# Decoder layer, 16 batches on one core: from batch 4 on, x is transposed by VectorE in 32x32 blocks and put together by way of DRAM

## The chip, the core and the metric

The kernel runs on one core of a Trainium2 chip. A core has five engines with an instruction queue each: TensorE (PE, matrix products; its weight loads are listed apart as PEld), VectorE (DVE), ScalarE (ACT), GpSimd (POOL) and SyncE (SP, which here only starts transfers). Sixteen DMA engines move data between DRAM and the on-chip memory SBUF. Matrix products end in PSUM, which has eight banks of 512 fp32 columns in this kernel's use. The metric is the time on the device in microseconds (us), the median of several runs.

## The reference, cut to what matters

x has shape (16, 512, 256), everything is fp32. Each batch goes through linear attention, cross attention to 64 context rows with softmax, and a routed expert layer, each with a residual and a layer norm. What the change touches is the first of these:

```python
q  = x + x @ Wq + bq
ks = x + x @ Wk[k] + bk[k]            # k = 0, 1
vs = x + x @ Wv[k] + bv[k]
state = prod_k (ks[k].T @ vs[k])      # per head, 16 heads of 16 channels
out = layernorm(q @ state) @ Wo + bo
x   = layernorm(x + out)
```

The expert layer keeps, for each of 8 experts, the first 1024 tokens of non-zero routing weight. With weights that are all positive these are batches 0 and 1, whose expert work is laid in the main part of the kernel. The last loop of the kernel takes up further batches if a count made on the chip asks for it.

## The kernel before, in words

A batch of x has 512 tokens and 256 channels. It is used in three forms.

- `gx` (`load_gram_x`, L293): tokens on partitions, four tiles of 128 tokens, with a column of ones set by POOL (L296). `gram` (L550) takes x.T x from it (L555, L560), which is a sum over tokens. The two gram blocks go to SBUF by `evac` (L182), which takes ACT (L186) and DVE (L188) in turn, and one block is transposed by TensorE (L573). Two buffers of `gx` exist; `gram` of batch b starts the load of batch b + 2.
- `xt` (`load_x`, L609): tokens on partitions again, one buffer, loaded at the start of `self_attention` (L614), used as the residual.
- `xT`: channels on partitions, 512 tokens in the free dimension, one buffer, which `zT` of the same batch shares. It is the weight operand of z = x m (L687), where m is Wq times the state of this batch.

`xT` is made from `xt` by `transposed` (L227): for each of two halves of the channels, four 128x128 TensorE transposes into one PSUM bank (L233), then one copy of 128x512 to SBUF. So a batch has eight transposes and two copies, one on ACT and one on DVE. The same helper makes `x1T` for the cross attention, and the transposed heads for the experts.

The order of all work is written out ahead by a planner. Generators stand for streams: grams, context, self attention, cross attention, routing, experts. A stream gives up its turn by `yield`; by `yield WAIT` it asks not to be called before the model's time at which what it has issued is done. `weave` (L1010) always calls the ready stream whose planned time is earliest. A stream's planned time moves with the TensorE time that it has spent, by the class `Model` (L28), which keeps a clock for each engine. One step of 78 us is planned for each batch (L1071, L1084); the gram of a batch is planned 3.8 steps ahead of its self attention (L1056 and L1071). Experts fill what is left (L1117). The resulting order is fixed for TensorE, VectorE, ScalarE and GpSimd by `in_order` (L1029). Each engine therefore runs its own list in order and waits by semaphores; SP likewise starts transfers in the order in which they are written.

All transfers of the kernel before are started by SP. Among those beside the change: the eight value blocks `vo` of a batch, 32 transfers in all (L781), of which the last two blocks are asked for while the product with the probabilities (`ps_x`, L834) runs; the loads of `gx` (L299) and `xt` (L611); the value store (L497).

`w_all` holds the routing weights of all batches; `ranks` writes a masked copy into `w_sel` (L910), which only the last loop reads.

Of the kernel before, what the change touches and what calls it, by code (L numbers as in the profile page):

```python
# [9 lines left out]
FP = mybir.dt.float32  # L10
# [17 lines left out]
class Model:  # L28
# [37 lines left out]
    def run(self):  # L66
# [4 lines left out]
        for ins in traced[self.seen:]:  # L71
# [4 lines left out]
            for made, used, l in ((1, 0, names[0]), (1, 1, names[1])):  # L76
                for n in l:
                    if kind == "InstDMACopy" and self.made.get(n, (0, 0))[1] == "SP":
                        continue
                    for known, book in ((made, self.made), (used, self.used)):  # L80
                        if known and n in book:
                            t, by = book[n]
                            at = max(at, t + (self.WIDE.get(by, 0.0) if by != engine else 0.0))
            if kind == "InstDMACopy":
                size = 4 * min(a.size() for l in aps for a in l)
                start = max(at, self.dma if now < 40 else 0.0)
                self.dma = start + size / 220e3
                done = self.dma + 2.0
            elif names[1]:
                start = max(at, self.free.get(engine, 0.0))  # L90
                done = self.free[engine] = start + self.duration(ins, kind, engine)
                if engine == "PE":
                    self.took += done - start
                else:
                    end = max(end, done + 0.15)
            else:
                continue
            for n in names[0] + names[1]:
                self.used[n] = max(self.used.get(n, (0.0, None)), (done, engine), key=lambda p: p[0])
            for n in names[1]:  # L100
                self.made[n] = (done, engine)
        self.seen, self.end = len(traced), end
# [14 lines left out]
def decoder_layer(  # L117
# [41 lines left out]
    HEAD_B = CAP // S  # L159
    GB = 2  # L160
    QB = 4
    CX = C + E
# [55 lines left out]
    NTT = B * NT  # L218
    w_sel = const.tile([P, NTT, E], FP, tag="w_sel", name="w_sel")
    n_i = const.tile([P, 1], I32, tag="n_i", name="n_i")  # L220
# [6 lines left out]
    def transposed(dst, src, view=lambda t: t, ones=False):  # L227


        for cc in range(NC):  # L230
# [3 lines left out]
            v = view(dst[:, cc, :])  # L234
            ps = ps if len(v.shape) == 2 else ps.rearrange("p (q t i) -> p q t i", q=NT, t=NT)
            if ones and cc == NC - 1:
                nc.vector.tensor_scalar(v, ps, not_last, ident[:, P - 1:P], ALU.mult, ALU.add)
            elif ones:
                nc.scalar.copy(v, ps)
            else:  # L240
                evac(v, ps)

    def moments(NT=NT):
# [28 lines left out]
    with ExitStack() as att:  # L272
# [19 lines left out]

        def load_gram_x(b, eng=nc.sync, pieces=1):  # L293

            t = gp.tile([P, NT, C + 1], FP, tag="gx", name="gx")
            nc.gpsimd.memset(t[:, :, C:], 1.0)  # L296
            n_ = NT // pieces
            for i in range(pieces):
                eng.dma_start(  # L299
                    out=t[:, i * n_:(i + 1) * n_, :C],  # L300
                    in_=x[b, i * n_ * P:(i + 1) * n_ * P, :].rearrange("(t p) c -> p t c", p=P),
                )
            return t

        gram_x = {0: load_gram_x(0, pieces=NT)}


# [142 lines left out]
        def context_keys():  # L450
# [27 lines left out]

            last = small.tile([P, NP], FP, tag="last", name="last")
            nc.vector.tensor_copy(last, xwq[:, :, C - 1])  # L480
# [69 lines left out]
        def gram(b, u4):  # L550
# [8 lines left out]
            for t in range(NT):  # L559
                nc.tensor.matmul(  # L560
                    ps[:, C + 1:C + P + 2], gx[:, t, P:C], gx[:, t, P:], start=(t == 0), stop=(t == NT - 1)
                )
            if b + 2 < B:
                gram_x[b + 2] = load_gram_x(b + 2)
            g = gp.tile([P, 4, P], FP, tag="g", name="g", bufs=5)
# [8 lines left out]
            evac(g[:, 3, :], ps[:, :P])  # L574
            grams[b] = g
            yield WAIT

# [28 lines left out]

        grams, sums = {}, {}

# [5 lines left out]
        def self_attention(b, done):  # L614
# [3 lines left out]
            sk = wk1.tile([P, K, NC, P], FP, tag="sk", name="sk")  # L618
            xT = wk1.tile([P, NC, S], FP, tag="xT", name="xT")
            gks = []  # L620

# [40 lines left out]
            nc.vector.scalar_tensor_tensor(state, state, STATE_SCALE, headmask, ALU.mult, ALU.mult)  # L662
            yield from until(lambda: made(xt))
            transposed(xT, xt)
            yield WAIT

# [13 lines left out]
            nc.scalar.copy(bq_state[:, :C], ps[:, :C])  # L680
            yield WAIT
            z = wk1.tile([P, NT, CX], FP, tag="z", name="z")
            mm = moments()
            for t in range(NT):
                ps = bank("ps_o")
                for cc in range(NC):
                    nc.tensor.matmul(  # L687
                        ps[:, :CX], xT[:, cc, t * P:(t + 1) * P], m[:, cc, :], start=(cc == 0), stop=(cc == NC - 1)
                    )
# [185 lines left out]
        def ranks():  # L875
# [33 lines left out]
            nc.vector.tensor_add(rank, rank, start)  # L909
            nc.vector.scalar_tensor_tensor(w_sel, rank, float(CAP), w_all, ALU.is_lt, ALU.mult)  # L910
            NB = B - HEAD_B
            least = small.tile([P, NB], FP, tag="least", name="least")
            nc.vector.tensor_reduce(
# [155 lines left out]
        def all_self_attention():  # L1069
            for b in range(B):  # L1070
                self_st.plan(SETUP + (b - 1) * STEP, STEP, 16.5)  # L1071
                yield from until(lambda: b in grams and sums[b // QB][1] and "rb" in cs and made(grams[b], sums[b // QB][1][0]))
                yield from self_attention(b, done)
# [86 lines left out]
    with tc.For_i(0, n, 1) as i:  # L1160
        acc = fw.tile([P, NT, C], FP, tag="acc", name="acc")
        nc.sync.dma_start(out=acc, in_=x2_rest[ds(i * S, S), :].rearrange("(t p) c -> p t c", p=P))
        wb = fw.tile([P, NT, E], FP, tag="wb", name="wb")
        nc.vector.tensor_copy(wb, w_sel[:, ds(i * NT + HEAD_B * NT, NT), :])
        aT = fw.tile([P, NC, S], FP, tag="aT", name="aT")
# [46 lines left out]
```

## Time and profile before

| | |
|---|---|
| median of 3 runs | 1387.47 us (1385.21 to 1389.51) |
| the profiled execution's own time | 1389.4 us |
| its span, first to last instruction | 1387.6 us |
| mean TensorE clock granted | 0.994 of full |
| ACT share of the span | 29% |
| DMA engines, mean busy share, all queues | about 41% |
| moved by DMA | 153.57 MB |

The profile shows one execution. An engine's busy time is the union of its instructions' durations. Consecutive matrix products overlap, so the duration of one is longer than the distance from its start to that of the next; that distance is read from the timeline. The chain of work that ended last is followed backward from the end: at each step to what released the instruction, or to its predecessor on the same engine.

### The profile page before, as it was taken

The numbers are of one execution on the slowest core, as the hardware profiler recorded it, in microseconds if no ns is written. First come the engines' busy times: TensorE is split into PE (matmuls) and PEld (weight loads), VectorE is DVE, ScalarE is ACT, GpSimd is POOL, SyncE is SP. The second block draws the span as 40 slices with busy tenths as digits, with TensorE's granted clock in tenths as the row PEclk, the third lists the DMA queues.
The fourth block names the chain that finished last, engine by engine and source line by source line (L and its number), as shares of the span: only waits on it lengthen the run. The fifth ranks groups of instructions, "written<-read, shape, count | busy, mean of one in ns | idle before, by whom it ended". The sixth has DMA issues, their size and how long they took to land.

```text
span 1387.6 us, 24209 instructions
## 1 busy us (share of the span) xinstructions
PE 1365.9 (98%) x9630; PEld 1077.9 (78%) x9630; DVE 850.7 (61%) x1957; ACT 402.2 (29%) x912; POOL 203.7 (15%) x140
## 2 busy tenths in 40 slices
PE   8999999999999999999999999999999999999997
PEld 5766576877878787878878787878888787878686
DVE  2445848466584848475584848475665939484744
ACT  1134224132232314142233323142323323232322
POOL 0001112112020111112020112112020202111200
PEclk9999999999999999999999999999999999999999
DMA  8657775511515153522606053513334061505211
GB/s 260 203 136 191 189 195 163 142 32 42 145 53 150 46 142 106 127 77 52 181 24 164 31 142 106 126 62 77 110 95 123 16 187 46 147 26 126 91 56 40
DMA packets 98372, 153.57 MB, mean 111 GB/s; under 512 B 15560, under 2 KB 70096, under 8 KB 98256
## 3 DMA queue, kind: packets, MB, share of 16 engines
q1 hardware_dynamic: 98256, 151.98, 40.1%
q8 instruction: 78, 1.28, 0.4%
q14 instruction: 38, 0.31, 0.1%
HBM read 114.71 MB, written 37.22 MB: 109 GB/s over the span
## 4 chain that ended last, share of the span: by engine, by line
PE 89%; DVE 5%; DMA 2%; SPq 1%; ACT 1%; issue 1%; ACTq 0%; DVEq 0%
PE ps_x L834 16%; PE ps_sim L814 15%; PE ps_e L963 15%; PE ps_h L946 15%; PE ps_gk L629 4%; PE ps_p L711 4%; PE ps_o L687 3%; PE ps_kv L437 3%; PE ps_t L233 2%; PE ps_kq L751 2%; PE ps_vo L492 2%; PE ps_s L641 2%; PE ps_g L555 2%; PE ps_zt L700 1%; PE ps_m L670 1%; PE ps_g L560 1%
## 5 line engine op out<-in xcount | busy, mean ns | idle before, releaser
L946 PE MATMUL ps_h<-head_T,wi 128*128 128x256 f32 x1024 | 239.1, 379 | 0.0
L834 PE MATMUL ps_x<-vo,pT 32*128 32x264 f32 x4096 | 234.9, 384 | 3.9 <-DVE pT L804 3.7
L814 PE MATMUL ps_sim<-kq,x1T 128*128 128x512 f32 x512 | 235.0, 593 | 0.0
L834 PEld LDWEIGHTS ps_x<-vo,pT 32*128 32x128 f32 x4096 | 211.5, 186 | 26.1 <-issue 5.6
L946 PEld LDWEIGHTS ps_h<-head_T,wi 128*128 128x128 f32 x1024 | 193.4, 190 | 38.8 <-issue 13.0
L802 POOL TENSOR_TENSOR s<-s,sm 128x1024 f32<-128x1024 f32 x64 | 121.7, 1901 | 539.8 <-DVE sm L801 501.4
L841 DVE TENSOR_TENSOR x<-ps_x,x 128x264 f32<-128x264 f32 x64 | 23.2, 426 | 226.3 <-PE ps_x L834 226.3
L822 ACT ACTIVATE s<-s 128x512 f32<-128x512 f32 x128 | 80.7, 630 | 276.1 <-DVE s L821 276.0
L814 PEld LDWEIGHTS ps_sim<-kq,x1T 128*128 128x128 f32 x512 | 94.5, 190 | 83.2 <-issue 74.5
L820 DVE TENSOR_REDUCE mx<-ps_sim 128x8 f32<-128x512 f32 x128 | 86.1, 673 | 42.0 <-PE ps_sim L814 41.6
L821 DVE TENSOR_TENSOR s<-ps_sim,mx 128x512 f32<-128x512 f32 x128 | 88.5, 692 | 4.4
L725 POOL TENSOR_TENSOR x<-x,bout 128x1056 f32<-128x1056 f32 x16 | 38.7, 2420 | 320.7 <-ACT hT L952 172.6
L804 DVE STREAM_TRANSPOSE pT<-s 128x1024 f32<-128x1024 f32 x64 | 78.6, 1228 | 7.0 <-POOL s L802 7.0
L952 ACT ACTIVATE hT<-ps_h 128x256 f32<-128x256 f32 x128 | 46.9, 376 | 119.9 <-PE ps_h L946 119.8
L701 ACT ACTIVATE zT<-ps_zt,shift,gain 128x512 f32<-128x512 f32 x32 | 23.2, 775 | 189.5 <-PE ps_zt L700 189.5
L800 DVE TENSOR_REDUCE sm<-s 128x16 f32<-128x1024 f32 x64 | 77.1, 1204 | 0.4 <-ACT s L822 0.4
L261 ACT ACTIVATE rstd<-bn_mv,eps 128x4 f32<-128x4 f32 (+1 forms) x70 | 20.7, 295 | 159.5 <-DVE bn_mv L250 156.0
L267 ACT ACTIVATE x<-x,off,rstd 128x264 f32<-128x264 f32 (+1 forms) x112 | 58.3, 591 | 29.3 <-DVE off L265 29.3
L687 PE MATMUL ps_o<-m,xT 128*128 128x264 f32 x256 | 66.7, 387 | 0.0
L954 DVE TENSOR_SCALAR hT<-ps_h 128x256 f32<-128x256 f32 x128 | 52.2, 409 | 22.5 <-PE ps_h L946 22.3
L711 PE MATMUL ps_p<-wo,zT 128*128 128x264 f32 x256 | 63.1, 387 | 0.0
L629 PE MATMUL ps_gk<-wk,g 128*128 128x256 f32 x256 | 61.2, 382 | 0.0
(174 smaller groups left out, 1897.4 us busy)
## 6 DMA issues: line engine op xcount, KB each, us to landing
vo<-vo_dram SPq DMA_DIRECT2D x512, 132.0 KB, 4.2
vo_dram<-vst SPq DMA_DIRECT2D x128, 132.0 KB, 2.4
xt<-in_x_dram SPq DMA_DIRECT2D x16, 512.0 KB, 4.0
wi<-L_ffn_experts_inter_dram SPq DMA_DIRECT2D x8, 1024.0 KB, 5.3
gx<-in_x_dram SPq DMA_DIRECT2D x15, 512.0 KB, 4.2
x_rest<-x SPq DMA_DIRECT2D x14, 512.0 KB, 3.1
out_dram<-x SPq DMA_DIRECT2D x14, 512.0 KB, 2.9
kT<-k_dram SPq DMA_DIRECT2D x8, 512.0 KB, 3.3
```

The costliest lines, as they stand in the source:

```text
L629: nc.tensor.matmul(ps[:, :C], blk, wk[:, j, k, :], start=(j == 0), stop=(j == NC - 1))
L687: nc.tensor.matmul(ps[:, :CX], xT[:, cc, t * P:(t + 1) * P], m[:, cc, :], start=(cc == 0), stop=(cc == NC - 1))
L711: nc.tensor.matmul(ps[:, :CX], zT[:, cc, t * P:(t + 1) * P], wo[:, cc, :], start=(cc == 0), stop=(cc == NC - 1))
L802: nc.gpsimd.tensor_mul(s, s, sm.unsqueeze(2).to_broadcast([P, NH, J]))
L804: nc.vector.transpose(probsT[:, :, t, :], s.rearrange("p h (a j) -> p (h a) j", a=2))
L814: nc.tensor.matmul(ps, x1T[:, cc, t * P:(t + 1) * P], kq[:, cc, hf * 512:(hf + 1) * 512], start=(cc == 0), stop=(cc == NC - 1),)
L820: nc.vector.tensor_reduce(mx[:, hs], sim, AX.X, ALU.max)
L821: nc.vector.tensor_sub(s[:, hs, :], sim, mx[:, hs].unsqueeze(2).to_broadcast([P, 8, J]))
L822: nc.scalar.activation(s[:, hs, :], s[:, hs, :], AF.Exp, scale=SCALE)
L834: nc.tensor.matmul(ps[q][:, :CX], probsT[pq, blk].rearrange("p t i -> p (t i)"), vos[c][pq, i, :], start=(c == 0 and i == 0), stop=(c == 7 ...
L946: nc.tensor.matmul(ps[:, :TB], wi[:, cc, f * P:(f + 1) * P], head_T[b][:, cc, t0 * P:t0 * P + TB], start=(cc == 0), stop=(cc == NC - 1),)
L963: nc.tensor.matmul(ps[:, :C], hT[f][:, t * P:(t + 1) * P], wo_[:, f, :], start=(f == 0), stop=(f == NF - 1),)
```

## The change

From batch 4 on (`FIRST = 4`), `xT` is no longer made by TensorE.

- `load_gram_x` loads `gx` with another order of the tokens: partition 32 i + j of tile q holds token 128 i + 32 q + j. It takes four transfers of 32 partitions each in place of one of 128.
- `gram` then calls `to_blocks`: four VectorE transposes of 128x256, each of which turns every 32x32 block in place and writes it into `xb`, a new buffer of 128x1024. Between them the stream gives up its turn for 1.3 us of the model's clock.
- One transfer, started by ACT, stores `xb` into a DRAM tile `x_blocks` of that batch (512 KB, 4 KB per partition).
- The load of `gx` for batch b + 2 is asked for after this, at the end of `gram`, and for all batches; before, it was asked for right after the gram's matrix products.
- `self_attention` starts with `from_blocks`: four transfers, started by ACT, read `x_blocks` into `xT`, each 32 partitions by four pieces of 1 KB. The eight transposes and two copies are left out.
- The planner's model gets a cost for transfers started by ACT (0.35 us of ACT, done after 5 us), self attention of a batch starts only when its `x_blocks` are made, and z waits in the model until `xT` is made.
- `xT` has the layout (token tile, channel half, 128) for all batches. For batches 0 to 3 the two copies write it with a stride.
- For space, `w_sel` is dropped: `ranks` masks the part of `w_all` after the head batches in place. Two small tiles keep one buffer.

```diff
-            if kind == "InstDMACopy":
+            if kind == "InstDMACopy" and engine == "Activation":
+                start = max(at, self.free.get(engine, 0.0))
+                self.free[engine] = start + 0.35
+                done = start + 5.0
+            elif kind == "InstDMACopy":
...
+    FIRST = 4
...
-    w_sel = const.tile([P, NTT, E], FP, tag="w_sel", name="w_sel")
...
+    def to_blocks(src):
+        xb = wk1.tile([P, NT, NC, NT, 32], FP, tag="xb", name="xb")
+        for q in range(NT):
+            nc.vector.transpose(
+                xb[:, :, :, q, :].rearrange("p k c j -> p c k j"),
+                src[:, q, :C].rearrange("p (c k j) -> p c k j", c=NC, j=32),
+            )
+            if q < NT - 1:
+                yield 1.3
+        return xb
+
+    def from_blocks(dst, there):
+        for k in range(NT):
+            nc.scalar.dma_start(
+                out=dst[k * 32:(k + 1) * 32].rearrange("i t c n -> i t (c n)"),
+                in_=there[:, :, k, :].rearrange("t i n -> i t n"),
+            )
...
+            pieces = 1 if 0 < b < FIRST else NT
             n_ = NT // pieces
             for i in range(pieces):
-                eng.dma_start(
-                    out=t[:, i * n_:(i + 1) * n_, :C],
-                    in_=x[b, i * n_ * P:(i + 1) * n_ * P, :].rearrange("(t p) c -> p t c", p=P),
-                )
+                if b < FIRST:
+                    eng.dma_start(
+                        out=t[:, i * n_:(i + 1) * n_, :C],
+                        in_=x[b, i * n_ * P:(i + 1) * n_ * P, :].rearrange("(t p) c -> p t c", p=P),
+                    )
+                else:
+                    eng.dma_start(
+                        out=t[i * 32:(i + 1) * 32, :, :C],
+                        in_=x[b, i * P:(i + 1) * P, :].rearrange("(q j) c -> j q c", j=32),
+                    )
...
-            if b + 2 < B:
-                gram_x[b + 2] = load_gram_x(b + 2)
             g = gp.tile([P, 4, P], FP, tag="g", name="g", bufs=5)
...
             grams[b] = g
+            if b >= FIRST:
+                yield WAIT
+                xb = yield from to_blocks(gx)
+                yield WAIT
+                x_blocks[b] = dram.tile([NT, 32, NT, NC * P], FP, tag=f"x_blocks{b}", name="x_blocks")
+                nc.scalar.dma_start(
+                    out=x_blocks[b].rearrange("t i k n -> (t i) (k n)"), in_=xb.rearrange("p k c q j -> p (k c q j)")
+                )
+            if b + 2 < B:
+                gram_x[b + 2] = load_gram_x(b + 2)
             yield WAIT
...
-            xT = wk1.tile([P, NC, S], FP, tag="xT", name="xT")
+            xT = wk1.tile([P, NT, NC, P], FP, tag="xT", name="xT")
+            if b >= FIRST:
+                from_blocks(xT, x_blocks.pop(b))
...
-            yield from until(lambda: made(xt))
-            transposed(xT, xt)
+            if b < FIRST:
+                yield from until(lambda: made(xt))
+                transposed(xT.rearrange("p t c n -> p c t n"), xt, lambda t: t)
             yield WAIT
...
+            yield from until(lambda: made(xT))
...
-                        ps[:, :CX], xT[:, cc, t * P:(t + 1) * P], m[:, cc, :], start=(cc == 0), stop=(cc == NC - 1)
+                        ps[:, :CX], xT[:, t, cc], m[:, cc, :], start=(cc == 0), stop=(cc == NC - 1)
...
-            nc.vector.scalar_tensor_tensor(w_sel, rank, float(CAP), w_all, ALU.is_lt, ALU.mult)
+            rest = slice(HEAD_B * NT, NTT)
+            nc.vector.scalar_tensor_tensor(
+                w_all[:, rest], rank[:, rest], float(CAP), w_all[:, rest], ALU.is_lt, ALU.mult
+            )
...
-                yield from until(lambda: b in grams and sums[b // QB][1] and "rb" in cs and made(grams[b], sums[b // QB][1][0]))
+                yield from until(
+                    lambda: b in grams and sums[b // QB][1] and "rb" in cs and made(grams[b], sums[b // QB][1][0])
+                    and (b < FIRST or b in x_blocks and made(x_blocks[b]))
+                )
```

More of the change, by code (lines that the diff above doesn't have):

```diff
@@ L98, in run @@
             for n in names[0] + names[1]:
-                self.used[n] = max(self.used.get(n, (0.0, None)), (done, engine), key=lambda p: p[0])
+                by = "SP" if kind == "InstDMACopy" else engine
+                self.used[n] = max(self.used.get(n, (0.0, None)), (done, by), key=lambda p: p[0])
             for n in names[1]:
-                self.made[n] = (done, engine)
+                self.made[n] = (done, "SP" if kind == "InstDMACopy" else engine)
         self.seen, self.end = len(traced), end
@@ L234, in transposed @@
             v = view(dst[:, cc, :])
-            ps = ps if len(v.shape) == 2 else ps.rearrange("p (q t i) -> p q t i", q=NT, t=NT)
+            if len(v.shape) > 2:
+                ps = ps.rearrange("p (q n) -> p q n", n=P) if len(v.shape) == 3 else ps.rearrange(
+                    "p (q t i) -> p q t i", q=NT, t=NT
+                )
             if ones and cc == NC - 1:
@@ L291, in decoder_layer, with load_gram_x @@
         wk2 = pool(att, "wk2", 2)
-        def load_gram_x(b, eng=nc.sync, pieces=1):
+        def load_gram_x(b, eng=nc.sync):
             t = gp.tile([P, NT, C + 1], FP, tag="gx", name="gx")
             nc.gpsimd.memset(t[:, :, C:], 1.0)
+            pieces = 1 if 0 < b < FIRST else NT
             n_ = NT // pieces
             for i in range(pieces):
-                eng.dma_start(
-                    out=t[:, i * n_:(i + 1) * n_, :C],
-                    in_=x[b, i * n_ * P:(i + 1) * n_ * P, :].rearrange("(t p) c -> p t c", p=P),
-                )
+                if b < FIRST:
[8 more added lines that the diff above has]
+                    )
             return t
-        gram_x = {0: load_gram_x(0, pieces=NT)}
+        gram_x = {0: load_gram_x(0)}
         early = wk1.tile([P, NC * GB * NP * P], FP, tag="kq", name="early")
@@ L475, in context_keys @@
             nc.sync.dma_start(out=xwq, in_=x_wq.rearrange("(r p) c -> p r c", p=P))
-            last = small.tile([P, NP], FP, tag="last", name="last")
+            last = small.tile([P, NP], FP, tag="last", name="last", bufs=1)
             nc.vector.tensor_copy(last, xwq[:, :, C - 1])
@@ L605, in grams_of @@
                     yield WAIT
-        grams, sums = {}, {}
+        grams, sums, x_blocks = {}, {}, {}
         def load_x(b):
@@ L618, in self_attention @@
             sk = wk1.tile([P, K, NC, P], FP, tag="sk", name="sk")
-            xT = wk1.tile([P, NC, S], FP, tag="xT", name="xT")
-            gks = []
+            xT = wk1.tile([P, NT, NC, P], FP, tag="xT", name="xT")
+            if b >= FIRST:
+                from_blocks(xT, x_blocks.pop(b))
             def g_times_wk(k):
@@ L909, in ranks @@
             nc.vector.tensor_add(rank, rank, start)
-            nc.vector.scalar_tensor_tensor(w_sel, rank, float(CAP), w_all, ALU.is_lt, ALU.mult)
+            rest = slice(HEAD_B * NT, NTT)
+            nc.vector.scalar_tensor_tensor(
+                w_all[:, rest], rank[:, rest], float(CAP), w_all[:, rest], ALU.is_lt, ALU.mult
+            )
             NB = B - HEAD_B
-            least = small.tile([P, NB], FP, tag="least", name="least")
+            least = small.tile([P, NB], FP, tag="least", name="least", bufs=1)
             nc.vector.tensor_reduce(
@@ L1071, in all_self_attention @@
                 self_st.plan(SETUP + (b - 1) * STEP, STEP, 16.5)
-                yield from until(lambda: b in grams and sums[b // QB][1] and "rb" in cs and made(grams[b], sums[b // QB][1][0]))
+                yield from until(
+                    lambda: b in grams and sums[b // QB][1] and "rb" in cs and made(grams[b], sums[b // QB][1][0])
+                    and (b < FIRST or b in x_blocks and made(x_blocks[b]))
+                )
                 yield from self_attention(b, done)
@@ L1163, in decoder_layer @@
         wb = fw.tile([P, NT, E], FP, tag="wb", name="wb")
-        nc.vector.tensor_copy(wb, w_sel[:, ds(i * NT + HEAD_B * NT, NT), :])
+        nc.vector.tensor_copy(wb, w_all[:, ds(i * NT + HEAD_B * NT, NT), :])
         aT = fw.tile([P, NC, S], FP, tag="aT", name="aT")
```

## The prediction

> **What bounds the kernel now.** I read the busy times first, then the chain that ended last, then the busy times by stage, then the timeline around one set of transposes.
>
> ```profile
> PE 1365.9 (98%) x9630; PEld 1077.9 (78%) x9630; DVE 850.7 (61%) x1957; ACT 402.2 (29%) x912; POOL 203.7 (15%) x140
> PE 89%; DVE 5%; DMA 2%; SPq 1%; ACT 1%; issue 1%; ACTq 0%; DVEq 0%
> ```
>
> TensorE is busy for all but 1387.6 - 1365.9 = 21.7 us, and 89% of the chain runs through it. The stages say where those 21.7 us lie (columns: stage, its length, busy us and instructions of PE, PEld, DVE, ACT, POOL, clock, DMA share, GB/s):
>
> ```profile
> 0.00:60.00 60.00, 53.90 (x215) 35.37 (x216) 17.01 (x48) 10.70 (x21) 2.46 (x16) 0.97 0.88 261
> 115.00:193.00 78.00, 76.20 (x447) 50.02 (x449) 53.26 (x113) 29.57 (x70) 12.58 (x9) 1.00 0.71 185
> 271.00:349.00 78.00, 74.75 (x529) 60.75 (x531) 48.24 (x102) 19.76 (x45) 12.48 (x7) 0.98 0.18 49
> 973.00:1051.00 78.00, 78.00 (x556) 63.34 (x555) 50.36 (x119) 22.49 (x50) 12.49 (x7) 1.00 0.42 117
> 1129.00:1207.00 78.00, 78.00 (x545) 63.05 (x544) 53.13 (x126) 24.03 (x54) 12.49 (x7) 1.00 0.40 111
> ```
>
> The start (6.1 us idle), two early stages (1.8 and 3.25) and the tail hold nearly all of it. From 349 to 1285 us, twelve stages of 78 us, TensorE has no idle time but 0.13 us. In the steady part, time is TensorE's work, and what is taken from it is won if nothing new makes it wait. The transposes of batches 4 to 15 lie in that part.
>
> **What is removed from TensorE.** Twelve batches of eight transposes, 96. A duration misleads here, because neighbours overlap; the distance between starts counts. The group before, the group itself and the group after, one batch of the steady part:
>
> ```profile
> 1228.97 1.89 PE L963 MATMUL ps_e<-wo__9602,hT 128*128 128x256 f32 x8
> 1230.70 1.04 PE L233 MATMUL ps_t<-ident,xt 128*128 128x128 f32 x8
> 1231.57 1.88 PE L814 MATMUL ps_sim<-kq,x1T 128*128 128x512 f32 x4
> ```
>
> From 1230.70 to 1231.57 is 0.87 us for eight, 0.109 us each; the set of batch 11 takes 932.54 to 933.41, the same. 12 x 0.87 = 10.4 us. Here a rule of the Trainium skill would give another sum: TensorE: Matmul & The Clock Gate, "Part 4: PE-mode transpose", puts a 128x128 transpose at about 275 ns inside a kernel. The row agrees with it as a duration:
>
> ```profile
> L233 PE MATMUL ps_t<-ident,xt x128: 272/273/273, 62.6 to 1231.5; 128*128 128x128 f32 x128
> L186 ACT COPY xT<-ps_t x16: 562/567/588, 63.2 to 1231.7; 128x512 f32<-128x512 f32 x16
> L188 DVE COPY xT<-ps_t x16: 678/684/685, 64.3 to 1232.3; 128x512 f32<-128x512 f32 x16
> ```
>
> 96 x 0.275 would be an estimate of 26.4 us. It counts 164 of the 273 ns that run under the neighbours, so I take 10.4. The copies that go with them, 12 on ACT (x 0.57 = 6.8 us) and 12 on DVE (x 0.68 = 8.2 us), are off the path: TensorE has other streams' work in its list right behind the transposes (the ps_sim above).
>
> **What is added to VectorE.** 48 block transposes of 128x256. The nearest row is the kernel's own block transpose, four times as wide, which also writes runs of 32 with a stride:
>
> ```profile
> L804 DVE STREAM_TRANSPOSE pT<-s 128x1024 f32<-128x1024 f32 x64 | 78.6, 1228 | 7.0 <-POOL s L802 7.0
> ```
>
> A quarter is 0.31 us; with the 0.15 us that a DVE copy of 128x1 takes as fixed part it is (1.23 - 0.15) / 4 + 0.15 = 0.42. I take 0.36: 1.44 us a batch, 17.3 us in all, net of the copies 9.1. Cover: DVE is idle 25 to 30 us in each steady stage, and the gram is planned 3.8 steps ahead of the use, so it may come late by whole steps. No cover where DVE itself is the path:
>
> ```profile
> 336.82 1.71 PE L834 MATMUL ps_x<-vo,pT 32*128 32x264 f32 x12 [3.25 <-DVE pT L804]
> ```
>
> Before this instruction DVE runs without a pause from about 320.5, and TensorE waits 3.25 us for the last probabilities. Grams 4 to 7 fall into the early stages, while self attention of batches 0 to 3 still has its copies. If the four transposes of one of them lie ahead of such a wait, it grows by up to 1.4 us: 0 to 1.4, I take 0.5.
>
> **What is added to ACT.** 12 x 5 = 60 transfers started from its queue. The trace has none on ACT; SP's are the nearest row:
>
> ```profile
> L299 SPq DMA_DIRECT2D gx<-in_x_dram x19: 368/396/1377, 0.8 to 822.6; - x19
> x_rest<-x SPq DMA_DIRECT2D x14, 512.0 KB, 3.1
> vo<-vo_dram SPq DMA_DIRECT2D x512, 132.0 KB, 4.2
> ```
>
> About 0.39 us each: 60 x 0.39 = 23.4 us, less 6.8 of copies, on an engine that is idle 53 us or more in each steady stage. The worst place is the start of self attention, four in a row, 1.6 us, ahead of exponentials (L822), expert activations (L952) and a norm. TensorE's cover is PSUM: eight banks, and an expert group takes two matrix products of 0.216 us (1.73 us for eight) per bank, so eight banks are 8 x 0.43 = 3.5 us. Cost 0; without that cover 12 x 1.6 = 19 us.
>
> New waits on ACT: the store waits for the four DVE transposes. The planner has the stream wait for them in the model, so ACT meets only what DVE lags behind the model; behind it wait the same exponentials and activations. The reads wait for a store issued steps earlier (3.1 us to landing for 512 KB) and for `zT` of the previous batch, whose products are over. 0 in the sum; the slower rival takes the other end.
>
> **DMA and SP.** Added: 12 x (512 KB written and 512 KB read) = 12.6 MB. Queue 1 moved 151.98 MB in 40.1% of the span, 273 GB/s while busy, so a stage gets 1.05 MB, 3.8 us of 78, on shares of 0.28 to 0.46. The first use of `xT` follows the start of self attention by tens of us (batch 11: `xt` is asked for at 906.0, L687 starts at 940.8); the reads need some 5 us. SP starts `gx` in four pieces rather than one: 3 x 0.39 = 1.2 us a batch. The Trainium skill speaks against that: DMA: Bandwidth & Descriptors, "Rules for kernel authors", calls splitting by partitions useless, since the halves share the same engines. By it, the split buys nothing and costs the issue time, 14 us of SP in all. What waits behind it are value loads: of those for the 7th block, SP starts the first 2.1 us into the product of 14.45 us (959.48 against 957.36), four take about 1.9 us (17.0 us for 32 x 0.53), landing takes 4.2, and the block is needed at 6/8 of 14.45 = 10.8 us. Margin 10.8 - 8.2 = 2.6 us, against 1.6 if four pieces of `gx` slip in ahead: hidden. Early it may not be: at 119 to 124 us the chain runs through SP's value stores, 0.6 us apiece, and two loads of `gx` may fall there. 0 to 2.4 us; I take 0.5. Asking for `gx` later costs nothing: the next gram of that buffer is two steps away; for batches 2 and 3, in the start, it could add to the wait of the start, 0 to 1 us, taken 0.
>
> `w_all` in place of `w_sel`: one operation of 0.69 us on fewer elements, 0. The z products read the same bytes. No new TensorE instruction appears.
>
> **The sum**, against the profiled execution: 1387.6 - 10.4 + 0.5 + 0.5 = 1378.2 us of span. That execution took 1389.4 us, 1.9 over the median; the difference of -9.4 on 1387.47 gives 1378 us.
>
> **Rivals.**
>
> *The gain is eaten by VectorE.* The transposes land ahead of the last probabilities in about half of the batches, where TensorE waits at `ps_x`: 6 x 1.44 = 8.6 us, so 1387.5 - 10.4 + 8.6 = 1385.7, no change. For: the wait of 3.25 us is this one, and DVE carries 50 of 78 us in every stage. Against: in all of the steady part there is no such wait, with the two copies of `xT` in the same stretch.
>
> *Slower: ACT stands at the store of `x_blocks`.* If DVE lags the model there, ACT waits in front of the exponentials and activations, TensorE runs out of banks after 3.5 us, and the rest is lost. It decides from 3.5 + 0.87 = 4.4 us of standing a batch; at 5.5 us it costs 12 x 2.0 = 24 us: 1387.5 - 10.4 + 24 = 1401. For: ACT's longest wait for DVE ahead of an exponential is 7.2 us now. Against: that one is not on the path, and the block transposes are issued one at a time with the planner's wait after the last.
>
> *More than the sum.* A new order closes the early waits (3.25 and 1.8 us) as well: 1387.5 - 10.4 - 5 = 1372. Nothing in the change aims at them.
>
> *It doesn't do what it says:* `xT` comes late from DRAM and z waits. The 35 us between speak against it; I put it with the slower rival.
>
> **How the numbers follow.** Forecast 0.72 (1375 to 1382: the sum with all gains at 10.4 and no loss is 1377; the upper ends of the costs, 1.4 + 2.4 + 1, give 1382); eaten 0.12 (1382 to 1391); slower 0.10; more 0.06. The range of 8 in 10 reaches from 1373 to 1386: the forecast, most of "more" and about half of "eaten". About 0.3%, 4.2 us, is what a measurement of this kernel tells from no change, so faster ends at 1383.3. Faster: 0.72 + 0.06 + 0.02 of "eaten" = 0.80; same 0.09; slower 0.11 (0.10 and 0.01 of the "eaten").
>
> **What would show it.** Right: 160 rather than 256 transposes of x and x1 together at L233 of before; TensorE busy about 10 us less, and still 78.0 of 78 us in the steady stages; block transposes of 128x256 at 0.31 to 0.42 us; ACT-started transfers at about 0.39 us; a last ps_x some 9 us earlier than 1324.3. Wrong: idle time of TensorE released by pT, hT or `xT` in the steady stages; ACT waiting for xb for several us; value blocks that TensorE waits for; a longer tail than the 8.8 us idle after 1345.

## The result, and where the profile after puts it

The changed kernel takes 1392.11 us (median, 1388.62 to 1395.97), the kernel before 1387.31 beside it: a ratio of 1.0043, 95% interval 1.0028 to 1.0058. It is slower by 4.8 us, where 9.4 us of gain was forecast. The range began at 1373 and ended at 1386.

The profiled execution of after has a span of 1389.1 us (1390.9 with what lies around it). The page's busy times and chain of after:

```profile
PE 1357.6 (98%) x9534; PEld 1071.3 (77%) x9534; DVE 854.6 (62%) x1993; ACT 397.4 (29%) x900; POOL 203.7 (15%) x140
PE 85%; DVE 8%; DMA 4%; SPq 1%; ACT 1%; issue 1%; POOL 0%; POOLq 0%; ACTq 0%
```

TensorE has its 96 instructions fewer and 8.3 us less of busy time, but idles 1389.1 - 1357.6 = 31.5 us where it idled 21.7. The chain has moved from PE (89% to 85%) to DVE (5% to 8%) and DMA (2% to 4%). The work was taken away; waits took its place. The stages of after say where (columns as in the prediction; first two stages of before that the prediction does not show, then after):

```profile
60.00:115.00 55.00, 54.51 (x303) 37.78 (x302) 27.59 (x69) 19.37 (x47) 2.50 (x3) 0.94 0.57 133
193.00:271.00 78.00, 76.80 (x679) 61.14 (x673) 45.88 (x106) 19.62 (x45) 12.68 (x9) 1.00 0.64 169
```

```profile
60.00:115.00 55.00, 52.74 (x281) 37.08 (x279) 26.40 (x64) 16.54 (x39) 2.53 (x2) 0.91 0.63 159
115.00:193.00 78.00, 74.71 (x395) 48.48 (x394) 55.40 (x122) 31.60 (x77) 12.60 (x8) 0.98 0.76 190
193.00:271.00 78.00, 72.23 (x654) 57.65 (x657) 46.10 (x103) 19.29 (x44) 12.58 (x8) 0.97 0.58 152
973.00:1051.00 78.00, 78.00 (x592) 63.21 (x585) 51.30 (x118) 19.16 (x44) 12.50 (x7) 1.00 0.55 148
```

Idle time grew by 1.8 us in 60 to 115 (0.49 before), by 1.5 us in the next stage and by 4.6 us in the one from 193 (1.2 before), with a lower granted clock in all three: together with the 1.0 us more of the first 60 us, 8.9 of the 9.8 us. A steady stage, the last line, is as full as before. (Over the twelve steady stages TensorE of after idles 1.1 us, before 0.13.) The addition that follows a batch's last ps_x marks how far a kernel is. From the timelines of DVE, third batch and last batch, first before and then after:

```profile
352.76 1.11 DVE L841 TENSOR_TENSOR x<-ps_x,x 128x264 f32<-128x264 f32 x3 [16.09 <-PE ps_x L834]
...
1338.79 1.11 DVE L841 TENSOR_TENSOR x<-ps_x,x 128x264 f32<-128x264 f32 x3 [14.01 <-PE ps_x L834]
```

```profile
361.84 1.11 DVE L890 TENSOR_TENSOR x<-ps_x,x 128x264 f32<-128x264 f32 x3 [14.60 <-PE ps_x L883]
...
1337.95 0.77 DVE L890 TENSOR_TENSOR x<-ps_x,x 128x264 f32<-128x264 f32 x2 [13.96 <-PE ps_x L883]
```

After is 9.1 us late at the third batch and 0.8 us ahead at the last, 9.9 us won between them. But the two kernels do not have the same work behind them at these marks. What is left after the last ps_x takes 2.3 us longer in after (1389.1 - 1337.95 against 1387.6 - 1338.79), with 12 more instructions of TensorE (192 against 180). And at the third batch after still has 16 small products to do that before has behind it:

```profile
395.57 1.84 PE L631 MATMUL ps_ks<-u,wk 128*128 128x4 f32 x16
```

They take 1.7 us up to the next start (397.28). So at like work, in these two executions, after wins 9.9 - 2.3 + 1.7 = 9.3 us from the third batch to the end, near the 10.4 of the sum, and it had lost 9.1 + 1.7 = 10.8 us before.

The added operations, by groups with shapes apart (durations in ns: least, median, longest):

```profile
L258 DVE STREAM_TRANSPOSE xb<-gx x48: 386/434/445, 133.6 to 1014.6; 128x256 f32<-128x256 f32 x48
L617 ACTq DMA_DIRECT2D x_blocks<-xb x12: 326/344/391, 154.4 to 1018.8; - x12
L268 ACTq DMA_DIRECT2D xT<-x_blocks x48: 309/442/787, 400.8 to 1214.0; - x48
```

### The profile page after: what moved, and what is told of

The parts are those of the page before. It is cut to its first block, busy times and chain, and to the rows that moved or that the text cites. A ratio compares the mean times of both kernels' runs of the same rounds, so it can differ in the third digit from the quotient of the medians.

```text
span 1389.1 us, 24194 instructions
## 1 busy us (share of the span) xinstructions
PE 1357.6 (98%) x9534; PEld 1071.3 (77%) x9534; DVE 854.6 (62%) x1993; ACT 397.4 (29%) x900; POOL 203.7 (15%) x140
## 4 chain that ended last, share of the span: by engine, by line
PE 85%; DVE 8%; DMA 4%; SPq 1%; ACT 1%; issue 1%; POOL 0%; POOLq 0%; ACTq 0%
PE ps_x L883 15%; PE ps_sim L863 14%; PE ps_h L998 14%; PE ps_e L1015 14%; PE ps_kv L475 4%; PE ps_p L760 4%; PE ps_gk L676 4%; PE ps_o L736 3%; DMA vo<-vo_dram 2%; PE ps_kq L800 2%; PE ps_vo L530 2%; PE ps_g L593 2%; PE ps_s L688 2%; PE ps_t L238 1%; DVE pT L853 1%; DVE sm L849 1%
```

## The experiments

Four reasons stood against each other. Theory A: the four transfers of `gx` delay SP's list in the start. B: the block transposes of grams 4 to 7 crowd VectorE in the early stages. C: the cost lies in every batch (ACT's transfers, DMA traffic). D: the later load of `gx` moves other work, by a POOL operation that then blocks VectorE. Differences below are of medians, against the kernel before beside each run unless another kernel is named. The intervals say how far to trust them: that of pieces_only is 5.7 to 9.8 us, that of gain_only -8.5 to -4.0.

| kernel | median us | before beside it | ratio, 95% interval |
|---|---|---|---|
| pieces_only | 1393.74 | 1387.12 | 1.0056, 1.0041 to 1.0071 |
| moved_only | 1389.81 | 1387.18 | 1.0023, 1.0012 to 1.0034 |
| gain_only | 1379.6 | 1387.12 | 0.9955, 0.9939 to 0.9971 |
| one_piece | 1386.75 | 1387.12 | 1.0001, 0.9987 to 1.0016 |
| first8 | 1386.46 | 1387.12 | 0.9999, 0.9988 to 1.0009 |
| first8_early | 1382.72 | 1387.18 | 0.9967, 0.9957 to 0.9977 |
| one_piece_early | 1386.6 | 1387.18 | 0.9999, 0.9987 to 1.0011 |
| one_piece_first8_early | 1383.78 | 1387.18 | 0.9973, 0.9963 to 0.9984 |
| no_early_blocks | 1379.01 | 1388.56 | 0.9943, 0.9924 to 0.9963 |
| no_early_store | 1385.87 | 1388.56 | 0.9990, 0.9977 to 1.0003 |
| one_piece_first6_early | 1388.92 | 1388.56 | 1.0001, 0.9989 to 1.0012 |
| after_no_early_blocks | 1388.16 | 1387.16 | 1.0005, 0.9992 to 1.0019 |

**pieces_only.** The kernel before, with `gx` of batches 4 to 15 in four transfers of 32 partitions, asked for where before asked for it. The lists of TensorE, VectorE, ScalarE and GpSimd are those of before word for word; only SP's differs.

```diff
-            for i in range(pieces):
+            for i in range(pieces if b < 4 else 0):
                 ...
+            for i in range(NT if b >= 4 else 0):
+                eng.dma_start(
+                    out=t[i * 32:(i + 1) * 32, :, :C],
+                    in_=x[b, i * P:(i + 1) * P, :].rearrange("(q j) c -> j q c", j=32),
+                )
```

> The kernel before, with one edit: from batch 4 on gx is loaded in four transfers of 32 partitions, at its old place. The lists of the four compute engines are those of before, word for word; only SP's list differs. Theory A (the start): the four pieces of gx for batches 4 and 5 push the loads of Wout behind eight key stores in SP's list, TensorE waits for Wout near 65 us as it does in the changed kernel; about 4 us slower, 1391. Theory B (crowded VectorE): the loss is made by the block transposes of grams 4 to 7, which are absent here; 1387 to 1388. Theory C (a cost spread over all batches: transfers on ACT, DMA traffic): 1387 to 1388.

Slower by 6.6 us: the largest single cost, from an edit that I had priced at a part of 0.5. The order in which SP starts its transfers, before and then pieces_only (timeline of SP: start, us, what it starts, how many):

```profile
35.72 0.37 SPq L299 DMA_DIRECT2D gx<-in_x_dram  x1
...
45.01 1.38 SPq L299 DMA_DIRECT2D gx<-in_x_dram  x1
...
49.07 0.50 SPq L520 DMA_DIRECT2D nato<-in_L_xattn_Wout_dram  x1
```

```profile
35.84 2.58 SPq L304 DMA_DIRECT2D gx<-in_x_dram  x4
...
44.88 1.93 SPq L304 DMA_DIRECT2D gx<-in_x_dram  x4
...
48.78 3.93 SPq L475 DMA_DIRECT2D k_dram<-st  x2
...
57.40 1.63 SPq L525 DMA_DIRECT2D nato<-in_L_xattn_Wout_dram  x2
```

SP spends 4.5 us on the two loads of `gx` rather than 1.75, but the first `nato` (Wout) starts 8.3 us later. SP's list is written in another order, in which the weights stand behind stores of keys. TensorE meets it at `ps_wo`. Pieces_only and then after:

```profile
66.08 1.06 PE L533 MATMUL ps_wo<-ident,nato 128*128 128x128 f32 x8 [0.63 <-DMA nato<-in_L_xattn_Wout_dram]
```

```profile
67.56 1.91 PE L566 MATMUL ps_wo<-ident,nato 128*128 128x128 f32 x8 [1.78 <-DMA nato<-in_L_xattn_Wout_dram]
```

The kernel before has no wait there. As TensorE's list is the same, its starts can be compared one by one: pieces_only falls behind by 0.9 us at `ps_wo`, by 0.5 near 108 us and by 1.8 near 126 us. At the last place four starts of `gx` stand ahead of value stores in SP's list, and VectorE's copy of values waits for a store (before; then three lines of pieces_only):

```profile
117.35 0.53 SPq L299 DMA_DIRECT2D gx<-in_x_dram  x1
```

```profile
118.71 1.96 SPq L304 DMA_DIRECT2D gx<-in_x_dram  x4
...
127.89 0.43 DVE L188 COPY vst<-ps_vo 128x264 f32<-128x264 f32 x1 [0.54 <-DMA vo_dram<-vst]
...
128.43 0.71 PE L497 MATMUL ps_vo<-xwoutT,st 64*128 64x264 f32 x2 [1.11 <-ACT g L186]
```

The profile puts TensorE's wait down to ACT's copy of `g`; in before the same product starts 1.2 us ahead of that copy, so VectorE's copy, which ends at 128.32, is the likelier releaser. So Wout is one part of the price and the value stores another. Pieces_only is 3.0 to 3.3 us late from the first batch to the last, with no further loss. The two profiled executions are 3.7 us apart and the medians 6.6, mainly because the one of before (1389.4) lies 2 us over its median; how the 6.6 divide is not shown.

**moved_only.** The kernel before, with only the load of `gx` for b + 2 moved to the end of `gram`. TensorE's, VectorE's and ScalarE's lists are those of before.

```diff
-            if b + 2 < B:
-                gram_x[b + 2] = load_gram_x(b + 2)
             g = gp.tile([P, 4, P], FP, tag="g", name="g", bufs=5)
             ...
             grams[b] = g
+            if b + 2 < B:
+                gram_x[b + 2] = load_gram_x(b + 2)
             yield WAIT
```

> The kernel before, with one edit: the load of gx for batch b + 2 is asked for at the end of gram rather than right after its matrix products. The lists of TensorE, VectorE and ScalarE are those of before; on POOL the memset of gx's column of ones comes later, on SP the load. Theory D (POOL and VectorE in each other's way): before, the memset holds POOL back near 250 us until a VectorE operation with two inputs in SBUF has passed; without it POOL's addition of 2.35 us starts first, that VectorE operation takes 2.2 us rather than 0.19, and TensorE waits some 2 us at the second ps_x and then runs some 4 us at a lowered clock: 3 to 4 us slower, 1390 to 1391. If the later load is harmless: 1387.

2.6 us slower, a little under what D expected. The same stretch of all engines' timeline, before and then moved_only:

```profile
250.43 0.19 DVE L860 TENSOR_TENSOR w_all<-w_all,rm 128x32 f32<-128x32 f32 x1
...
250.59 0.10 POOL L296 MEMSET gx<- 128x4 f32 x1 [0.45 <-PE ps_g L560]
...
250.79 2.35 POOL L705 TENSOR_TENSOR xt<-xt,bo 128x1024 f32<-128x1024 f32 x1
...
252.74 2.51 PE L834 MATMUL ps_x<-vo,pT 32*128 32x264 f32 x40 [0.49 <-DVE pT L804]
```

```profile
247.42 2.34 POOL L705 TENSOR_TENSOR xt<-xt,bo 128x1024 f32<-128x1024 f32 x1
247.62 2.20 DVE L860 TENSOR_TENSOR w_all<-w_all,rm 128x32 f32<-128x32 f32 x1
...
251.91 3.40 PE L834 MATMUL ps_x<-vo,pT 32*128 32x264 f32 x56 [2.47 <-DVE off L265]
```

In before, POOL's memset of `gx` waits for the gram's products (0.45 us), which holds POOL's addition back until the router's subtraction on VectorE is done. With the memset gone from there, the addition starts 0.2 us ahead of the subtraction, which then takes 2.20 us rather than 0.19. A norm's operation (`off`) stands behind it in VectorE's list, and ps_x waits 2.47 us for that. Start by start, moved_only loses 2.2 us at this ps_x and nothing behind it.

In the changed kernel the order of this stretch is another, and the collision takes another form: the subtraction (L909) has its 0.19 us, but the addition just ahead of it in the router takes 1.41 rather than 0.24 us behind POOL's, and ps_x waits 1.32 us for `off`:

```profile
257.30 1.41 DVE L907 TENSOR_TENSOR w_all<-x_head,rb 128x32 f32<-128x32 f32 x1
```

So 2.6 us is the price in the order of before; what it is in after was not measured by itself.

**gain_only.** The changed kernel without what it adds, apart from the transfers that read `xT`. The transposes of batches 4 to 15 are left out, `xT` is read from x as it lies, and `gx` comes in one transfer at the old place.

```diff
-            if b >= FIRST:
-                yield WAIT
-                xb = yield from to_blocks(gx)
-                ...
+            yield WAIT
 ...
-                from_blocks(xT, x_blocks.pop(b))
+                from_blocks(xT, x[b].rearrange(...))
```

> Leaves part of the computation out: from batch 4 on there are no TensorE transposes, no block transposes and no store; xT is read by the same four ACT-started transfers, but straight from x in DRAM (the same bytes, so xT is not the transpose). gx is one transfer, at its old place. What is left is the removal and the reads. If 10.4 us is the right size of the removal and the reads on ACT cost nothing: 1377 (theories A and B). Theory C in the form that ACT's four reads or their traffic cost time: 1385 or more.

It wins 7.5 us, not 10.4. Part of what is missing is work that the transposes had covered. From its list of waits (us in all, times, longest):

```profile
PE ps_m L710 <- DVE state L701: 2.5, 4, 0.7
```

The transposes stood between the making of `state` and its use. Without them ps_m waits for it in four batches, 2.5 us in all, a wait that before does not have. In the profiled execution TensorE idles 24.9 us where before's idles 21.7, which is of the size of the difference between 10.4 and 7.5. But this belongs to the order of gain_only. The same wait in after:

```profile
PE ps_m L718 <- DVE state L709: 0.3, 1, 0.3
```

From the third batch to the end gain_only wins 6.1 us in its profiled execution, after 9.3. So 7.5 is not what the removal is worth in after.

**one_piece.** The changed kernel with tokens dealt as 4 p + q, so that one transfer fills `gx`.

```diff
-                    eng.dma_start(
-                        out=t[i * 32:(i + 1) * 32, :, :C],
-                        in_=x[b, i * P:(i + 1) * P, :].rearrange("(q j) c -> j q c", j=32),
-                    )
+                    eng.dma_start(out=t[:, :, :C], in_=x[b].rearrange("(p q) c -> p q c", q=NT))
 ...
-        xb = wk1.tile([P, NT, NC, NT, 32], FP, tag="xb", name="xb")
+        xb = wk1.tile([P, NT, NC, 32, NT], FP, tag="xb", name="xb")
```

> The changed kernel with another order of tokens in gx (partition p of tile q holds token 4p + q), so that gx is one transfer again from batch 4 on; the block transposes write with a stride of four elements, all else stays. SP's list in the start is that of before again. Theory A: the 4 us of the start come back; with them alone, 1388. If A is the whole of the early loss, 1378. Theory B: 1391 to 1392, the early waits from 200 to 350 us stay. Theory C: 1392.

1386.75, 5.4 us below the changed kernel: with the four transfers goes about as much as pieces_only had lost. It is no clean undoing: its block transposes write every fourth element, and each takes 0.64 us rather than 0.43.

**first8.** The changed kernel with FIRST = 8: no early gram has blocks or pieces, and 3.5 us of saving are given up (32 transposes).

```diff
-    FIRST = 4
+    FIRST = 8
```

> The changed kernel with FIRST = 8: batches 4 to 7 are transposed by TensorE again, so the early stages have no block transposes and gx of batches 4 to 7 is one transfer. 8 x 0.87 = 7.0 us are taken from TensorE rather than 10.4. Theories A and B both: the early loss is gone, 1380 to 1382. Theory C: the costs scale with the batches, 8/12 of the measured +4.8: 1390.

It ended between the two, at 1386.46. A and B had promised 1380 to 1382, C 1390. Its timeline shows the same subtraction at 2.20 us behind POOL's addition, with ps_x waiting 2.48 us; this is where theory D came from.

**first8_early.** FIRST = 8, and for b < 8 the load of `gx` where before has it.

```diff
+            if b + 2 < B and b < FIRST:
+                gram_x[b + 2] = load_gram_x(b + 2)
             g = gp.tile([P, 4, P], FP, tag="g", name="g", bufs=5)
 ...
-            if b + 2 < B:
+            if b + 2 < B and b >= FIRST:
                 gram_x[b + 2] = load_gram_x(b + 2)
```

> FIRST = 8, and for batches below 8 the next gx is asked for at its old place, so that all lists up to the gram of batch 8 are those of before, POOL's memsets included. Removed from TensorE: 7.0 us. Theory D: 3 to 4 us better than with FIRST = 8 alone (1386.5): 1382 to 1383. If the loss of that kernel lies in the steady part (waits of 2.4 us there): 1386.

1382.72: 3.7 us better than first8, and faster than both kernels, by 0.33% (0.23 to 0.43) against before. The 64 transposes taken out are 7.0 us by the sum; of the 2.5 missing, TensorE idles 2.3 from 739 to 817 us (waits at ps_e, ps_kq and ps_x), where before has no idle time. The subtraction is back at 0.19 us, and the stage from 193 has before's idle time:

```profile
193.00:271.00 78.00, 76.61 (x667) 60.99 (x660) 46.02 (x106) 19.74 (x45) 12.70 (x9) 1.00 0.66 169
```

**one_piece_early and one_piece_first8_early.** one_piece, with the loads of the first batches early; then the same with FIRST = 8.

```diff
+            if b + 2 < B and b < FIRST:
+                gram_x[b + 2] = load_gram_x(b + 2)
```

> The changed kernel (FIRST = 4) with gx in one transfer and, for batches 0 to 3, the next gx asked for at its old place. Theory D plus A: 1386.8 of the one-transfer kernel less 0 to 4 us: 1383 to 1386. Theory B (block transposes of grams 4 to 7 crowd VectorE near 200 to 350 us) says that most of the early loss stays, since those are all there: 1386.

> FIRST = 8, gx in one transfer, the next gx at its old place for batches below 8. As with four transfers, if the four transfers of gx cost nothing once the start is over: 1382 to 1383. If each costs SP or the value loads something: 1 to 2 us better than with four transfers.

With blocks from batch 4 the early load wins nothing over one_piece. That says little about D: with FIRST = 4 only grams 0 to 3 load early, while the memset that held POOL back at 250 us in before is that of batch 9, asked for by gram 7; and the subtraction has its 0.19 us here, as in after. From batch 8 it gives 1383.78, as good as first8_early within the intervals. So four transfers cost nothing measurable once the start is over, which is against C, and batches 4 to 7, with blocks and late loads, cost more than the 3.5 us that they save.

**no_early_blocks and no_early_store.** one_piece_early, where batches 4 to 7 read `xT` from x as it lies: first without the blocks and stores of grams 4 to 7, then with the blocks and without the stores.

```diff
-            if b >= FIRST:
+            if b >= 8:
                 yield WAIT
                 xb = yield from to_blocks(gx)
```

```diff
                 yield WAIT
-                x_blocks[b] = dram.tile(...)
-                nc.scalar.dma_start(...)
+                if b >= 8:
+                    x_blocks[b] = dram.tile(...)
+                    nc.scalar.dma_start(...)
```

> one_piece_early without the block transposes and stores of grams 4 to 7: batches 4 to 7 read xT from x itself, so their xT has the right bytes in number and the wrong values; nothing is transposed for them on any engine. Theory B (the blocks of grams 4 to 7 cost the early stages about 6.3 us, by the difference of two runs): 1386.6 - 6.3 = 1380.3, 1379 to 1382. Rival (the missing gain has another cause, which both of those runs shared in unequal parts, such as the reads of xT, the layout of xT or the steps that the early stages run without TensorE's transposes): stays at 1385 or above.

> As one_piece_early, with the block transposes of grams 4 to 7 kept and their store left out: batches 4 to 7 read xT from x itself (wrong values). It splits theory B: if the 16 block transposes on VectorE are what costs, 1386.6 stays, 1385 to 1388; if the store from ScalarE's queue and the wait for it at the start of self attention is, it falls to that of no_early_blocks, about 1380.

1379.01 and 1385.87, on the same chip, with intervals that do not meet. The two kernels differ by the 16 block transposes and by the turns that gram gives up between and around them: together these make the 6.9 us. So early blocks cost, as theory B says. Whether by VectorE's time or by the longer stream, which orders everything anew, is not separated: no run keeps the turns and leaves the transposes out. What the stores add, by the ratios 0.9999 of one_piece_early and 0.9990, lies inside the intervals. What TensorE waits for in one_piece_early (its timeline from 180 to 345):

```profile
184.33 1.09 PE L748 MATMUL ps_zt<-ident,z 128*128 128x128 f32 x8 [1.78 <-ACT vst L192]
...
209.15 0.33 PE L238 MATMUL ps_t<-ident,x 128*128 128x128 f32 x1 [1.82 <-ACT x L297]
...
250.36 0.33 PE L608 MATMUL ps_gt<-ident,g 128*128 128x128 f32 x1 [2.12 <-ACT g L192]
...
334.31 0.33 PE L608 MATMUL ps_gt<-ident,g 128*128 128x128 f32 x1 [2.45 <-DVE g L194]
```

None of these four waits stands in no_early_blocks, where grams lie as in before:

```profile
205.86 0.33 PE L608 MATMUL ps_gt<-ident,g 128*128 128x128 f32 x1
...
210.11 0.33 PE L608 MATMUL ps_gt<-ident,g 128*128 128x128 f32 x1
```

What these waits show is a new order more than a crowded VectorE. ps_gt of gram 6 has moved from 210 to 250 us, that of gram 7 from 326 to 334, just ahead of ps_x of the second and third batch (253.75 and 340.68), so that TensorE, whose list is fixed, stands for the eviction of `g`. ps_gt of gram 5 has come earlier, from 206 to 185.

**one_piece_first6_early.** one_piece_early with FIRST = 6.

> one_piece_early with FIRST = 6: the same, with batches 4 and 5 left to TensorE, so 1.74 us of the saving are given up and the blocks of grams 4 and 5 with them. If each of the four grams costs the same (6.3 / 4 = 1.6 us), 1386.6 + 1.74 - 3.15 = 1385.2; if the cost is that of the first one or two, which fall into the first stages, about 1382; if of grams 6 and 7, 1388.

1388.92, a ratio of 1.0001: the cost is not spread evenly over the four grams, and leaving two of them out gave nothing. The number is near the case of grams 6 and 7 (1388), but that reading is not safe: in its timeline of TensorE the second ps_x waits 5.20 us for an operation of the router, where no_early_blocks waits 2.48 for a norm:

```profile
255.11 15.95 PE L882 MATMUL ps_x<-vo,pT 32*128 32x264 f32 x256 [5.20 <-DVE rm L911]
```

So a new order around one place can cost nearly as much as the blocks, and how the cost divides over the four grams stays open.

**after_no_early_blocks.** The last doubt was whether the early blocks cost as much in the changed kernel itself, where each takes 0.43 and not 0.64 us. The edit is that of no_early_blocks, made in the changed kernel.

> The changed kernel, with its loads of gx as they are (four transfers, late), without the block transposes and stores of grams 4 to 7: batches 4 to 7 read xT from x itself (wrong values). Its own block transposes take 0.43 us, those of one_piece_early 0.64 us, so the 7.6 us that leaving them out gave there (1386.6 to 1379.0) need not hold here. By the sum of the single runs (pieces 6.6, late loads 2.6, removal -7.5, after 4.8 above before) about 3 us are left for the blocks: 1392.1 - 3 = 1389, 1388 to 1390.5. If the early blocks cost in the changed kernel what they cost there, 1392.1 - 7.6 = 1384.5, and the four transfers and late loads cost less together than one by one. If they cost nothing, 1392.

1388.16, 4.0 us under the changed kernel. The parts, each from a run of its own, come near the result: pieces +6.6, late loads +2.6, early blocks +4.0, transposes gone -9.3 by the profile of after (-7.5 by gain_only), in all +3.9 (+5.7) against +4.8 measured. This is no proof that they are the parts of after: each is uncertain by 2 us or so, and they are not independent. The subtraction of 2.20 us that makes moved_only slow is in after_no_early_blocks and in no_early_blocks too, and not in after.

Against theory C stands no_early_blocks: it has the block transposes and stores of batches 8 to 15, gain_only has none, and its ratio is no higher (0.9943 against 0.9955). What the reads of `xT`, which both have, cost by themselves was not measured.

One thing cuts across all four theories. The granted clock was 0.988 to 0.991 in the nine runs of after, 0.9893 in the mean, and 0.9952 in the mean of the 159 runs of before beside the experiments. Within those 159 runs, all of one kernel, 0.001 of clock goes with 1.2 us. By that rate, an estimate, 7 us of after's time go with its lower clock. This is an upper end: in the profiled pair (0.990 against 0.994, 4.6 us by the rate) TensorE's busy time shows 2.1 us. Without the early blocks the clock is 0.9921, by the rate up to 3.4 of the 4.0 us. It is no fifth theory, since three of the low stretches of after stand behind new waits (last section), but it says in what form part of the loss was paid.

## Why the prediction was wrong, point by point

The step that failed is the price of the first 350 us: 0.5 for SP, 0.5 for VectorE, nothing for the later load and nothing for the clock, 1.0 in all. The profile of after lost 10.8 there, at like work.

- **"12 x 0.87 = 10.4 us".** Mechanism right, size nearly: after wins 9.3 us from the third batch on, and another 1.0 is new idle time in the steady stages. That gain_only wins only 7.5 shows a risk that I had not asked about: the transposes also covered VectorE's work on `state`, and in another order ps_m waits for it (2.5 us there, 0.3 in after).
- **"SP starts gx in four pieces rather than one ... 0 to 2.4 us; I take 0.5".** The term that was furthest off: 6.6 us. I had priced four starts at 0.39 us each in the steady part, and two loads ahead of the value stores near 120 us. That place did cost 1.8 us in pieces_only, within the 0 to 2.4. What I had not seen is that SP's list in the start is written in another order: Wout came 8.3 us later and ps_wo waited, 0.6 us in pieces_only and 1.8 in after. The Trainium skill's rule that I quoted there (DMA: Bandwidth & Descriptors, "Rules for kernel authors") calls such a split useless; the runs agree (four transfers in first8_early, one in one_piece_first8_early, no difference beyond the intervals), and one_piece recovered 5.4 us. Its price was not the issue time alone, by which I had counted it.
- **"Asking for gx later costs nothing".** 2.6 us in moved_only; in after not measured alone. I had asked who needs `gx` and not what else goes with the load: a memset on POOL that held back a POOL addition.
- **VectorE early, "0 to 1.4, I take 0.5".** 4.0 us. I had looked for blocks ahead of the 3.25 us wait for probabilities. That wait did not grow (in after, ps_x at 347.30 waits 1.05 us for pT); it was the grams that moved, and waits at ps_gt, ps_zt and ps_t that came.
- **No term for the clock.** 8.3 us of busy time went where 10.4 had been removed, and the granted clock was lower in the stages with new waits (0.91, 0.98 and 0.97 for 0.94, 1.00 and 1.00). Between 2.1 us, by busy time, and 7, by the estimate above, are paid in this form.
- **Right:** the steady part is won (9.3 us) with TensorE at 77.3 to 78.0 of 78; 160 transposes of x and x1 remain; ACT's starts take 0.34 and 0.44 us for an expected 0.39, and no instruction of ACT stands at the store; no engine has a wait for `xT` from DRAM. The block transpose takes 0.43 us, just over the upper bound of 0.42 and not 0.36. The last ps_x ends 0.8 us earlier, not the 9 us named as a sign.
- **The rivals.** "Gain eaten by VectorE" had VectorE's new work right and the place wrong: not in half of the batches but in four grams. "ACT stands at the store" fell. No rival spoke of the first 60 us, and my bounds of the start (2.4 + 1) were drawn from issue times, so the range could not reach 1392.

## What to carry to other kernels

An edit for the steady part is paid for wherever its code also runs: ask of each moved or split operation what it does in the start and the ramp, and begin it later if nothing is lost (FIRST = 8 with early loads turned +4.8 us into -4.5). Compare the granted clocks of two kernels as well as their idle times. A list of transfers or instructions that a program writes out is not the old list plus the new entries; compare the order around the late weights first. Of work that is removed, ask what it covered, and of an operation that is moved, which queue it held back.

## What the runs showed of the hardware

**A short wait of TensorE can be paid twice.** In after, TensorE waits 1.82 us, and the gram's products behind it take nearly twice the time (timelines of TensorE, after and then before):

```profile
215.76 0.33 PE L238 MATMUL ps_t<-ident,x 128*128 128x128 f32 x1 [1.82 <-ACT x L297]
...
217.91 3.54 PE L593 MATMUL ps_g<-gx 128*128 128x257 f32 x8
```

```profile
210.34 1.98 PE L555 MATMUL ps_g<-gx 128*128 128x257 f32 x8 [0.17 <-ACT vst L186]
```

The granted clock is 0.72 from 216 to 220 us in after and 1.00 in those 4 us of before. It was low behind two more new waits of after: 0.57 from 190 to 194 us (a wait of 2.22 us) and 0.58 from 340 to 344 (2.46). But the length of the wait does not decide it. In the same execution a wait of 2.12 us ends at 256.98 and the clock stays full (stages of after):

```profile
216.00:220.00 4.00, 3.49 (x13) 2.61 (x13) 3.90 (x11) 2.17 (x6) 1.43 (x2) 0.72 0.98 259
256.00:260.00 4.00, 2.07 (x9) 1.51 (x9) 3.07 (x8) 0.99 (x4) 2.66 (x3) 1.00 0.02 4
260.00:264.00 4.00, 3.63 (x64) 3.37 (x68) 0.82 (x5) 2.22 (x5) 0.00 (x0) 1.00 0.12 35
```

The same wait at ps_x, 2.47 or 2.48 us, was followed by a clock of 1.00 in moved_only, where a lowered one was expected, and of 0.66 (252 to 256 us) in first8. The Trainium skill (TensorE: Matmul & The Clock Gate, "Why this matters for your kernels") puts the idle gap that returns the array to half rate at about 3 us; here shorter ones were followed by a low clock, and some were not. Half clock also comes without a wait: from 68 to 72 us it is 0.50 in before, while TensorE is busy throughout. In moved_only, with the same list on TensorE, it is 1.00 there, and that execution gains 2.7 us between 68 and 73 us. What decides it stays open.

**The scatter of one kernel goes with its clock.** The 159 runs of before range from 1381.82 to 1393.87 us with granted clocks of 0.999 and 0.991 at the two ends; the means at 0.993, 0.995 and 0.998 are 1390.0, 1387.0 and 1384.2 us.

**VectorE stands for the whole of a POOL addition.** The subtraction of 128x32 with two SBUF inputs takes 0.19 us, or 2.20 when POOL's addition (2.34 us) began 0.2 us earlier; it ends 0.06 us after it. The Trainium skill (SBUF — State Buffer, "Who interferes with whom") says that a VectorE instruction with two SBUF inputs contends with a GpSimd one that reads SBUF, that the shared ports are an exclusive lock, and that the order of issue decides who waits; the trace agrees. What decides who is second is a few tenths of a microsecond: the subtraction began 0.36 us ahead of the addition in before, and 0.2 us behind it in moved_only.
